# An attention and mixture-of-experts kernel: row-half pairs for the last 64 units of routed tiles, another place for transposes and for normalised rows

## The chip, the cores and the metric

The kernel runs on one core of one Trainium2 chip. The metric is the device time of one execution in microseconds (us); lower is better. The time before is 720.77 us, the median of three runs (720.6 to 722.7).

## The reference

The input x has 16 sequences of 100 tokens with 256 channels (1600 tokens), and each sequence has a context of 361 tokens with 192 channels. All is fp32.

```
x = x + attention(layernorm(x), context)       16 heads of 64; q = x Wq, k, v = context Wkv
                                               softmax(q k^T / 8) v, then Wproj and bproj
h = layernorm(x)
swiglu(h, w1, w2, w3) = (silu(h w1^T) * (h w3^T)) w2^T          704 units
shared = swiglu(h, sw1, sw2, sw3)
p, e   = the largest of 7 sigmoid scores of the router, and its expert
x = x + 0.5 / (0.5 + p) * shared + p / (0.5 + p) * swiglu(h, ew1[e], ew2[e], ew3[e])
```

## The kernel before, in words

**Order of work.** TensorE's order is written out by hand for the whole kernel, and in the attention part those of ScalarE (ACT), VectorE (DVE) and the DMA queue of SyncE (SP) too. Behind the attention, ACT, DVE, SP and GpSimd (POOL) are ordered by a scheduler. All matmul results land in one ring of eight PSUM banks.

**Attention** (L857 to L922) is a loop over 32 steps, s = 2b + g, for batch b and half g of the heads. A step has four score pairs (L688): two 64-row matmuls side by side, whose maxima DVE takes (L701), whose exponentials ACT makes (L704), and which DVE turns in blocks of 32 (L717, for the pair before). Between the score pairs of a step stand the products of keys and values of the next batch (L611). At the end of a step with g = 0 come, in this order on TensorE: the "fillers" (the projection L792 of a finished tile of 128 tokens, and the router's product L245), two units of q (L587) and the products of probabilities with values of batch b-1 (L760).

**Layer norms** run in parts that are spread over the loop. `layer_norm` (L170) gives parts (moments of each tile, roots, and L192, which writes a normalised tile `xn`) and a function `turn`, which transposes the tiles on TensorE (L212) and copies them on ACT into `xT` (L215). One part is taken by `part()` after each of the turned score pairs, so four in a step: after the score pairs i = 1, 2 and 3 are issued and at the step's end. When a group's parts are through, its `turn` is put on the queue `turns`. Groups of tiles: (0, 1) and (2..5) ahead, (6, 7, 8) and (9..12) from step 6 and 9 on for q; and then, for the second half of the layer (`keep`), (0, 1, 2), (3, 4, 5), (6, 7, 8) as the attention finishes them. In the kernel before, `turns` are taken at the beginning of a step with g = 0, behind its first score pair (L899). All normalised tiles share four buffers `xn`.

**Loads.** The context of batch b+2 is loaded at the end of step (b, 1) into one of two buffers `cT` (L917). `load_shared` (L223) loads the first two shared weights `w13_sb` in steps 10 to 13.

**Shared expert** (L984 to L1013): after the attention, `hidden` (L424) and `down` (L493). `down` already takes tiles in pairs for the last 64 units: two matmuls of 64 rows, in the upper and lower half of the array, one for each tile (L499).

**Routed experts** (L1028 to L1093). Tokens are sorted by expert into slot tiles of 128; the number of tiles is found at run time (15 here), and `tc.Switch` branches to code for that number. `fetch` (L949) loads the weights of a slot tile three tiles ahead, 2176 KB. `run(k)` makes on TensorE 8 of 11 unit blocks (L1020, 32 instructions), the transposes of tile k+1 (L979), the last 3 blocks (12 instructions), and then `finish(k-1)`: six matmuls of 128 x 256 (L1032, 12 instructions), the sixth for the last 64 units with 64 rows of zeros, then DVE's sum L1036 and POOL's scattered write L1037. Before the Switch stand `turn(0)`, ahead of the last `down`, and the first 8 blocks of tile 0 (L1087).

Of the kernel before, what the change touches and what calls it, by code (L numbers as in the profile page):

```python
# [14 lines left out]
F32 = mybir.dt.float32  # L15
# [3 lines left out]
ALU = mybir.AluOpType  # L19
# [3 lines left out]
B, LQ, C = 16, 100, 256  # L23
LKV, CTX = 361, 192
H, DK = 16, 64
I, E = 704, 7
P = 128
N = B * LQ
# [18 lines left out]
SINGLE = tuple(t for t in range(NT) if not any(t in p for p in PAIRS))  # L47
NS = (N - E) // P + E
NF = (N + P - 1) // P
WE = 2 * 2 * I + (NI + 1) * C  # L50
QG = 2


# [11 lines left out]
def xattn_moe(  # L65
# [11 lines left out]
    w13: bass.AP,  # L77
    w2: bass.AP,
    wex: bass.AP,
    out: bass.AP,  # L80
):
    nc = tc.nc
# [42 lines left out]
    def bank():  # L125
        return ps.tile([P, 512], F32, tag="mm", name="mm")
# [40 lines left out]

    biases = deque()

    def layer_norm(tiles, keep=False):  # L170


        n = len(tiles)
        of, xns = {}, []

        def moments(i):
            if i == 0:
                of["mv"] = small.tile([P, 4, 2], F32, name="mv")
                of["rstd"] = small.tile([P, 4], F32, name="rstd")
            st = small.tile([P, 6], F32, name="st")  # L180
            nc.vector.bn_stats(st, acc[:, tiles[i], :])
            nc.vector.bn_aggr(of["mv"][:, i, :], st)

        def roots():
            rstd = of["rstd"]
            nc.vector.tensor_scalar(rstd[:, :n], of["mv"][:, :n, 1], EPS, None, ALU.add)
            nc.gpsimd.tensor_tensor(rstd[:, :n], rstd[:, :n], power[:, :n], ALU.pow)

        def normalise(i):
            t = tiles[i]  # L190
            xn = small.tile([P, C], F32, name="xn", bufs=4)
            nc.vector.tensor_scalar(  # L192
                xn,
                acc[:, t, :],
                of["mv"][:, i, 0:1],
                of["rstd"][:, i : i + 1],
                ALU.subtract,
                ALU.mult,
            )
            if keep:  # L200
                nc.sync.dma_start(xn_d[t * P : t * P + rows(t), :], xn[: rows(t), :])
            else:
                biases.append(t)
            xns.append(xn)

        def turn():
            for i in range(0, n, 2):
                tr = bank()
                m = min(2, n - i)
                for o in range(m):  # L210
                    for k in range(2):
                        nc.tensor.transpose(  # L212
                            tr[:, ds((k * m + o) * P, P)], xns[i + o][:, ts(k, P)], ident
                        )
# [296 lines left out]
    with ExitStack() as attn:  # L511
# [34 lines left out]
        def load_later(s):  # L546

            if 1 < s < 4:
                m = ts(s - 2, NCH // 2)
                nc.sync.dma_start(  # L550
                    wp_sb[:, m], wproj.rearrange("(m p) c -> p m c", p=P)[:, m]
                )
            if s == 3:
                nc.sync.dma_start(rb_sb, rbias.to_broadcast([P, E]))
                nc.sync.dma_start(rw_sb[:, :, :E], rwT.rearrange("(k p) e -> p k e", p=P))
            if s == 4 or s == 7:
                load_x(GROUPS[s // 3 + 1])
            if s == 6 or s == 9:
                normalised(GROUPS[s // 3])
            if 10 <= s < 14:  # L560
                load_shared(s - 10)
            if s in (2 * B - 3, 2 * B - 2):
                load_shared(s - 2 * B + 7)

# [234 lines left out]
        turns, fillers, norms = deque(), deque(), deque()  # L799

        def normalised(g, keep=False):
            parts, turn = layer_norm(g, keep)
            norms.extend(parts)


            def turned():
                turn()
                if keep:
                    fillers.append(lambda: norms.extend(router(g)))

            norms.append(lambda: turns.append(turned))
# [31 lines left out]
        pairs = key_pairs(0)  # L843
        product(pairs)
        product(pairs)
        parts, turn_first = layer_norm(FIRST)
        for one in parts:
            one()
        product(pairs)
# [12 lines left out]
        for s, (b, g) in enumerate(steps):  # L862
# [25 lines left out]
            for i in range(n2):  # L888
                exponentials, then = scores(b, g * n2 + i)
                if puts:  # L890
                    puts.popleft()()
                exponentials()
                if turning:
                    turning(tb)
                    part()
                turning = then
                for _ in range(-(-len(pairs) // (n2 - i))):
                    product(pairs)
                while g == i == 0 and turns:  # L899
                    turns.popleft()()  # L900
            if puts:
                puts.popleft()()
            if g == 0:
                while fillers:
                    fillers.popleft()()
                for _ in range(min(2, len(qs))):
                    qs.pop(0)()
# [6 lines left out]
                    after_values()  # L914
                finished(b - 1)
            held.append(moved(tb))
            if g == NG - 1 and b + 2 < B:  # L917
                cTs[b + 2] = load_ctx(b + 2)
            if g == NG - 1:
                host(b)  # L920
# [21 lines left out]

    NW = 4
    wexs = [ew.tile([P, WE], F32, name=f"wex{i}") for i in range(NW)]
    hTs = [ew.tile([P, NI + 1, P], F32, name=f"hgT{i}") for i in range(2)]
    for hT in hTs:
        nc.gpsimd.memset(hT[HALF:, NI, :], 0.0)

    def fetch(k):  # L949

        e = nc.sync.value_load(e_at[:, k : k + 1], min_val=0, max_val=E - 1)
        nc.sync.dma_start(wexs[k % NW], wex[ds(e, 1)].rearrange("o p w -> (o p) w"))

    NX = 4
    xgs, bgs = [], []
    for i in range(NX):
        xgs.append(ew.tile([P, C], F32, name=f"xg{i}"))
        bgs.append(ew.tile([P, C], F32, name=f"bg{i}"))
        nc.gpsimd.memset(xgs[i], 0.0)
        nc.gpsimd.memset(bgs[i], 0.0)  # L960

    def index(k):
        return bass.IndirectOffsetOnAxis(ap=slot_token[:, k : k + 1], axis=0)

    def gather_into(to, of, k):

        nc.gpsimd.indirect_dma_start(
            out=to[k % NX],
            out_offset=None,
            in_=of,  # L970
            in_offset=index(k),
            bounds_check=N - 1,
            oob_is_err=False,
        )
# [9 lines left out]
    with tc.tile_pool(name="hs", bufs=1) as hs:  # L984
# [4 lines left out]
                piece()  # L989
            return hT  # L990

        parts, turn_last = layer_norm(GROUPS[-1], keep=True)
        for one in parts:
            one()
        hT = run_hidden(GROUPS[1])
# [13 lines left out]
        down([(6, hT2, 0), (7, hT2, 1)])  # L1009
        down([(12, hT3, 3)])  # L1010
        down([(9, hT3, 0), (10, hT3, 1)])
        ahead = turn(0)
        down([(8, hT2, 2), (11, hT3, 2)])  # L1013
    hp = ctx.enter_context(tc.tile_pool(name="hp", bufs=2))

# [9 lines left out]
                    stop=(j == 1),  # L1025
                )

    def finish(k, hT, bg):  # L1028
        w = wexs[k % NW]
        y = bank()  # L1030
        for c in range(NI + 1):
            nc.tensor.matmul(  # L1032
                y[:, :C], hT[:, c, :], w[:, ds(4 * I + c * C, C)], start=(c == 0), stop=(c == NI)
            )
        o = hp.tile([P, C], F32, name="o")
        nc.vector.scalar_tensor_tensor(o, y[:, :C], slots[:, k, 1:2], bg, ALU.mult, ALU.add)  # L1036
        nc.gpsimd.indirect_dma_start(  # L1037
            out=out,
            out_offset=index(k),
            in_=o,  # L1040
            in_offset=None,
            bounds_check=N - 1,
            oob_is_err=False,
        )

    def first_products(k, xgT):
        pa, pb = bank(), bank()
        w = wexs[k % NW]
        products(pa, xgT, w, [i * P for i in range(NI - 1)])
        products(pb, xgT, w, [I + HALF + i * P for i in range(NI - 1)])  # L1050
        return pa, pb

    def run(k, state, tiles):


        xgT, last, made = state
        w, hT = wexs[k % NW], hTs[k % 2]
        pa, pb = made or first_products(k, xgT)
        pc = bank()
        n = (NI - 1) * P  # L1060
        s = sp.tile([P, n], F32, name="sg")
        nc.scalar.activation(s, pa[:, :n], AF.Silu)
        nc.vector.tensor_tensor(
# [8 lines left out]
        nc.scalar.activation(s[:, :P], pc[:, :P], AF.Silu)  # L1072
        nc.scalar.activation(s[:HALF, P:], pc[P - HALF :, ts(1, P)], AF.Silu)
        nc.vector.tensor_tensor(hT[:, NI - 1, :], pc[:, ts(2, P)], s[:, :P], ALU.mult)
        nc.vector.tensor_tensor(hT[:HALF, NI, :], pc[:HALF, ts(1, P)], s[:HALF, P:], ALU.mult)
        if last is not None:
            finish(*last)
# [4 lines left out]
        return ahead, (k, hT, bgs[k % NX]), None  # L1082

    n = nc.values_load(e_at[:, NS:], min_val=0, max_val=NS - NF)
    for k in range(NX - 1):
        gather_into(bgs, base_d, k)
    first = ahead, None, first_products(0, ahead)  # L1087

    for extra in tc.Switch(n, NS - NF + 1):
        then = first  # L1090
        for k in range(NF + extra):
            then = run(k, then, NF + extra)
        finish(*then[1])  # L1093


# [52 lines left out]
```

## Time and profile before

| what | value |
| --- | --- |
| median of 3 runs | 720.77 us |
| the profiled execution: own time | 721.24 us |
| its span, first to last instruction | 719.4 us (mean granted TensorE clock 0.995) |
| TensorE (PE) busy | 707.9 us |
| DVE, ACT, POOL busy | 420.5, 280.7, 197.3 us |
| products and steps of the attention | 4.2 to 512.9 us |
| shared expert, sort | to 595.7 us |
| routed experts | 595.7 to 714 us |

How to read it: the timeline lists instructions of one engine in order, merged where alike; its columns are the start in us, the time from there to the end of the last one, engine, line, operation, the tiles, and the count. A part in square brackets is idle time before it and what ended that. Matmuls are pipelined, so the time that a group takes from its neighbours is the distance from its start to the next start. One fp32 matmul is two instructions on TensorE.

### The profile page before, as it was taken

Reading aid. Unit: us, or ns where it says so; the run is one execution under the profiler, and the core shown is the slowest. Engines: PE = TensorE matmul, PEld = TensorE weight load, DVE = VectorE, ACT = ScalarE, POOL = GpSimd, SP = SyncE. Lnnn points to the kernel's source line nnn. Section 1 sums busy time; section 2 is a strip of 40 time slices with the busy share of each in tenths; the row PEclk is TensorE's granted clock in tenths of the full one; section 3 lists DMA queues with packets and bytes.
Section 4 is the critical chain, followed back from the end, with each engine's and each line's share of the span. In section 5 each row is a group of like instructions: output and inputs, shape, how many; then the busy total and the mean of one; then the engine's idle time right before and its main releaser. Section 6 shows DMA issues by size and latency. Waiting matters only on the chain. (4 is left out here: it accounts for less than half of the span.)

```text
span 719.4 us, 14826 instructions
## 1 busy us (share of the span) xinstructions
PE 707.9 (98%) x5192; PEld 510.3 (71%) x5192; DVE 420.5 (58%) x1100; ACT 280.7 (39%) x793; POOL 197.3 (27%) x417
## 2 busy tenths in 40 slices
PE   9999999999999999999999999999999998999996
PEld 6556667667575766757577576755866578999996
DVE  2777766867687576876778778677247222122121
ACT  2564563534545263453644636453022111111110
POOL 4142422322342222323223322233010104343321
PEclk9999999999999999999999999999999999999999
DMA  7055756454474543537354473555104912998860
GB/s 260 23 140 157 178 128 159 95 140 125 106 204 127 166 109 96 139 88 197 93 136 124 109 181 83 142 129 143 52 26 155 382 34 58 326 348 333 309 249 23
DMA packets 55979, 109.23 MB, mean 152 GB/s; under 512 B 28681, under 2 KB 37964, under 8 KB 53972
## 3 DMA queue, kind: packets, MB, share of 16 engines
q1 hardware_dynamic: 45252, 81.79, 37.1%
q0 software_dynamic: 10352, 25.98, 13.8%
q8 instruction: 44, 0.72, 0.4%
q14 instruction: 43, 0.35, 0.2%
q10 hardware_dynamic: 288, 0.39, 0.2%
HBM read 60.81 MB, written 5.35 MB: 92 GB/s over the span
## 5 line engine op out<-in xcount | busy, mean ns | idle before, releaser
L704 ACT ACTIVATE at<-mm,nm 128x361 f32<-128x361 f32 x256 | 142.0, 561 | 173.4 <-DVE nm L701 173.2
L738 POOL DMA_DIRECT2D aT<-tb x256 | 126.1, 500 | 296.7 <-PE mm L760 104.6
L701 DVE TENSOR_REDUCE nm<-mm 128x1 f32<-128x361 f32 x256 | 123.5, 523 | 60.1 <-PE mm L688 59.3
L717 DVE STREAM_TRANSPOSE tb<-at 128x384 f32<-128x384 f32 x256 | 132.9, 558 | 4.5
L611 PE MATMUL mm<-cT,wk_sb 64*128 64x361 f32 x768 | 125.8, 467 | 0.5 <-DMA cT<-in_ctxT 0.4
L611 PE MATMUL mm<-wv_sb,cT 64*128 64x512 f32 (+1 forms) x552 | 126.2, 589 | 0.0
L611 PEld LDWEIGHTS mm<-cT,wk_sb 64*128 64x128 f32 x768 | 75.7, 188 | 45.7 <-issue 5.0
L688 PE MATMUL mm<-kT,qT 64*128 64x361 f32 x512 | 99.2, 479 | 1.7 <-ACT at L704 1.7
L611 PEld LDWEIGHTS mm<-wv_sb,cT 64*128 64x128 f32 (+1 forms) x552 | 53.7, 185 | 53.1 <-issue 43.1
L1020 PE MATMUL mm<-xgT,wex 128*128 128x128 f32 x660 | 78.3, 275 | 0.0
L1020 PEld LDWEIGHTS mm<-xgT,wex 128*128 128x128 f32 x660 | 76.9, 192 | 1.0 <-issue 0.3
L688 PEld LDWEIGHTS mm<-kT,qT 64*128 64x128 f32 x512 | 48.8, 188 | 35.8 <-issue 8.9
L760 PE MATMUL mm<-aT,v 128*64 128x100 f32 (+1 forms) x1472 | 72.5, 251 | 0.5 <-DMA aT<-tb 0.4
L760 PEld LDWEIGHTS mm<-aT,v 128*64 128x64 f32 (+1 forms) x1472 | 67.2, 135 | 4.9 <-issue 3.0
L424 PE MATMUL mm<-xT,w_sb 128*128 128x384 f32 (+1 forms) x176 | 60.9, 503 | 0.0
L424 PEld LDWEIGHTS mm<-xT,w_sb 128*128 128x128 f32 x176 | 32.9, 190 | 26.1 <-issue 8.5
L704 ACT ACTIVATION_READ_ACCUMULATOR at<-mm,nm 128x1 f32 x256 | 50.7, 198 | 0.0
L587 PE MATMUL mm<-xT,wq_sb 128*128 128x200 f32 x256 | 46.9, 336 | 0.0
L587 PEld LDWEIGHTS mm<-xT,wq_sb 128*128 128x128 f32 x256 | 43.4, 190 | 4.0 <-issue 1.5
L792 PE MATMUL mm<-wp_sb,resT 128*128 128x256 f32 x192 | 44.8, 386 | 0.0
L651 ACT COPY kT<-mm 128x361 f32<-128x361 f32 x64 | 29.4, 461 | 39.2 <-PE mm L611 39.2
L792 PEld LDWEIGHTS mm<-wp_sb,resT 128*128 128x128 f32 x192 | 35.9, 191 | 10.3 <-issue 2.5
(154 smaller groups left out, 558.9 us busy)
## 6 DMA issues: line engine op xcount, KB each, us to landing
wex<-in_wex SPq DMA_DIRECT2D x15, 2176.0 KB
aT<-tb POOLq DMA_DIRECT2D x256, 80.2 KB, 3.3
aT<-tb SPq DMA_DIRECT2D x256, 80.2 KB
over<-row SPq DMA_DIRECT2D x64, 100.0 KB
cT<-in_ctxT SPq DMA_DIRECT2D x10, 576.0 KB
cT<-in_ctxT SPq DMA_DIRECT2D x5, 541.5 KB
xn_d<-xn SPq DMA_DIRECT2D x12, 128.0 KB
base_d<-acc SPq DMA_DIRECT2D x12, 128.0 KB
```

Of the source, the lines that this page charges most:

```text
L424: nc.tensor.matmul(to[:, :n], w13_sb[:, k, ds(at, P)], xT[:, k, ds(g[0] * P, n)], start=(k == 0), stop=(k == 1),)
L587: nc.tensor.matmul(pq[:, o, :], wq_sb[:, u, k, ts(o, P)], xT[:, k, ts(g, QG * LQ)], start=(k == 0), stop=(k == 1),)
L611: nc.tensor.matmul(to[o][:height, :width], *operands(o, k), start=(k == 0), stop=(k == NR - 1),)
L651: nc.scalar.copy(kT[:, c, :], to[0][:, :LKV])
L688: nc.tensor.matmul(sc[o][:, :LKV], qTs[b // QG][r, c, ts(b % QG, QB), :], kTs[b][c // 4][r, c % 4, :], start=True, stop=True,)
L701: nc.vector.tensor_reduce(nm[:, o : o + 1], sc[o][:, :LKV], AX.X, ALU.max, negate=True)
L704: nc.scalar.activation(at[:, o, :LKV], sc[o][:, :LKV], AF.Exp, bias=nm[:, o : o + 1], accum_out=sums[:, o : o + 1],)
L717: nc.vector.transpose(tb[:, :, :, o, i * QR : i * QR + 32].rearrange("p j k n -> p k j n"), at[:, o, :].rearrange("p (k j n) -> p k j n", ...
L738: queue.dma_start(aT[ts(j, 32), i].rearrange("p k o n -> p (k o n)"), tb[ts(i, 32), j].rearrange("p k o n -> p (k o n)"),)
L760: nc.tensor.matmul(av[ts(o, DK), i, :], v[:n, ds((2 * c + o) * DK, DK)], aT[:n, :, j, o, ts(i, QR)], start=(j == 0), stop=(j == NJ - 1),)
L792: nc.tensor.matmul(pp[:r, :C], resT[:, c, QP : QP + r], wp_sb[:, c, :], start=(c == 0), stop=(c == NCH - 1))
L1020: nc.tensor.matmul(to[:, ts(o, P)], w[:, ds(j * 2 * I + u, P)], xgT[:, j, :], start=(j == 0), stop=(j == 1),)
```

## The change

1. **Last 64 units of the routed tiles.** `WE` loses one block of 256 columns; the last 64 rows of w2 come in a tensor of their own, `wlast`, twice (both halves of the partitions), by a second DMA in `fetch`. The hidden values of the last 64 units go to `tails`, an even tile into partitions 0 to 63, an odd one into 64 to 127. `finish` makes five blocks and holds an even tile back (unless it is among the last three) until the next tile's five blocks are made; then both tails are multiplied, 64 rows each, and both tiles written.
2. **Transposes in the attention.** `turns` are taken at the end of a step with g = 0, behind the last score pair and ahead of the fillers, but for batch 1, where the place stays.
3. **Normalised tiles for q** are written into `w13_sb`; the four `xn` buffers are left for the kept ones. The loads of `w13_sb` move from steps 10 to 13 to steps 20 to 23.
4. **Context loads** stand at the end of step (b, 0), for b = 0 at (b, 1).
5. **Switch.** `turn(0)` moves behind the last `down` and the load of the tile count; the first 8 blocks of tile 0 move into the branches.

```
-    def layer_norm(tiles, keep=False):
+    def layer_norm(tiles, place=None):
...
-            xn = small.tile([P, C], F32, name="xn", bufs=4)
+            xn = small.tile([P, C], F32, name="xn", bufs=4) if keep else place[:, ts(i, C)]
...
-            if 10 <= s < 14:
-                load_shared(s - 10)
+            if 20 <= s < 24:
+                load_shared(s - 20)
...
+        places = [w13_sb[:, i % 2, :] for i in (1, 0, 1, 0)]
...
-                while g == i == 0 and turns:
+                if b == 1 and g == i == 0:
                     turns.popleft()()
             if puts:
                 puts.popleft()()
             if g == 0:
+                while turns:
+                    turns.popleft()()
                 while fillers:
                     fillers.popleft()()
...
-            if g == NG - 1 and b + 2 < B:
+            if g == (NG - 1 if b == 0 else 0) and b + 2 < B:
                 cTs[b + 2] = load_ctx(b + 2)
...
+        nc.sync.dma_start(wlasts[k % NL], wlast[ds(e, 1)].rearrange("o p w -> (o p) w"))
...
-        ahead = turn(0)
         down([(8, hT2, 2), (11, hT3, 2)])
...
-    def finish(k, hT, bg):
+    def finish(k, hT, tiles):
         w = wexs[k % NW]
         y = bank()
-        for c in range(NI + 1):
+        for c in range(NI):
             nc.tensor.matmul(
-                y[:, :C], hT[:, c, :], w[:, ds(4 * I + c * C, C)], start=(c == 0), stop=(c == NI)
+                y[:, :C], hT[:, c, :], w[:, ds(4 * I + c * C, C)], start=(c == 0), stop=False
             )
+        waiting.append((k, y))
+        if k % 2 == 0 and k < tiles - 3:
+            return
+        for at, y in waiting:
+            r = ts(at % 2, HALF)
+            nc.tensor.matmul(
+                y[:, :C], tails[at // 2 % 2][r], wlasts[at % NL][r], start=False, stop=True
+            )
+        while waiting:
+            at, y = waiting.pop(0)
...
+            nc.vector.scalar_tensor_tensor(o, y[:, :C], slots[:, at, 1:2], bg, ALU.mult, ALU.add)
...
-        nc.vector.tensor_tensor(hT[:HALF, NI, :], pc[:HALF, ts(1, P)], s[:HALF, P:], ALU.mult)
+        tail = tails[k // 2 % 2][ts(k % 2, HALF)]
+        nc.vector.tensor_tensor(tail, pc[:HALF, ts(1, P)], s[:HALF, P:], ALU.mult)
...
-    first = ahead, None, first_products(0, ahead)
+    first = turn(0), None
```

More of the change, by code (lines that the diff above doesn't have):

```diff
@@ L49 @@
 NF = (N + P - 1) // P
-WE = 2 * 2 * I + (NI + 1) * C
+WE = 2 * 2 * I + NI * C
 QG = 2
@@ L79, in xattn_moe @@
     wex: bass.AP,
+    wlast: bass.AP,
     out: bass.AP,
@@ L168, in xattn_moe @@
     biases = deque()
-    def layer_norm(tiles, keep=False):
+    def layer_norm(tiles, place=None):
         n = len(tiles)
+        keep = place is None
         of, xns = {}, []
@@ L801, in normalised @@
         def normalised(g, keep=False):
-            parts, turn = layer_norm(g, keep)
+            parts, turn = layer_norm(g, None if keep else places.pop(0))
             norms.extend(parts)
@@ L845, in xattn_moe @@
         product(pairs)
-        parts, turn_first = layer_norm(FIRST)
+        places = [w13_sb[:, i % 2, :] for i in (1, 0, 1, 0)]
+        parts, turn_first = layer_norm(FIRST, places.pop(0))
         for one in parts:
@@ L944, in xattn_moe @@
     wexs = [ew.tile([P, WE], F32, name=f"wex{i}") for i in range(NW)]
-    hTs = [ew.tile([P, NI + 1, P], F32, name=f"hgT{i}") for i in range(2)]
-    for hT in hTs:
-        nc.gpsimd.memset(hT[HALF:, NI, :], 0.0)
+    hTs = [ew.tile([P, NI, P], F32, name=f"hgT{i}") for i in range(2)]
+    tails = [ew.tile([P, P], F32, name=f"tail{i}") for i in range(2)]
+    NL = 6
+    wlasts = [ew.tile([P, C], F32, name=f"wlast{i}") for i in range(NL)]
     def fetch(k):
@@ L952, in fetch @@
         nc.sync.dma_start(wexs[k % NW], wex[ds(e, 1)].rearrange("o p w -> (o p) w"))
+        nc.sync.dma_start(wlasts[k % NL], wlast[ds(e, 1)].rearrange("o p w -> (o p) w"))
     NX = 4
[L955 to L960, printed above, removed]
+    xgs = [ew.tile([P, C], F32, name=f"xg{i}") for i in range(NX)]
+    bgs = [ew.tile([P, C], F32, name=f"bg{i}") for i in range(NX + 1)]
+    for one in xgs + bgs:
+        nc.gpsimd.memset(one, 0.0)
     def index(k):
@@ L967, in gather_into @@
         nc.gpsimd.indirect_dma_start(
-            out=to[k % NX],
+            out=to[k % len(to)],
             out_offset=None,
@@ L990, in run_hidden @@
             return hT
-        parts, turn_last = layer_norm(GROUPS[-1], keep=True)
+        parts, turn_last = layer_norm(GROUPS[-1])
         for one in parts:
@@ L1026, in products, with run @@
                 )
-    def finish(k, hT, bg):
+    waiting = []
+    def finish(k, hT, tiles):
         w = wexs[k % NW]
         y = bank()
-        for c in range(NI + 1):
+        for c in range(NI):
             nc.tensor.matmul(
-                y[:, :C], hT[:, c, :], w[:, ds(4 * I + c * C, C)], start=(c == 0), stop=(c == NI)
+                y[:, :C], hT[:, c, :], w[:, ds(4 * I + c * C, C)], start=(c == 0), stop=False
             )
[L1035 to L1048, printed above, removed]
+        waiting.append((k, y))
[8 more added lines that the diff above has]
+            at, y = waiting.pop(0)
+            o = hp.tile([P, C], F32, name="o")
+            bg = bgs[at % len(bgs)]
+            nc.vector.scalar_tensor_tensor(o, y[:, :C], slots[:, at, 1:2], bg, ALU.mult, ALU.add)
+            nc.gpsimd.indirect_dma_start(
+                out=out,
+                out_offset=index(at),
+                in_=o,
+                in_offset=None,
+                bounds_check=N - 1,
+                oob_is_err=False,
+            )
+    def run(k, state, tiles):
+        xgT, last = state
+        w, hT = wexs[k % NW], hTs[k % 2]
+        pa, pb, pc = bank(), bank(), bank()
+        n = (NI - 1) * P
         products(pa, xgT, w, [i * P for i in range(NI - 1)])
         products(pb, xgT, w, [I + HALF + i * P for i in range(NI - 1)])
[L1051 to L1060, printed above, removed]
         s = sp.tile([P, n], F32, name="sg")
@@ L1074, in run @@
         nc.vector.tensor_tensor(hT[:, NI - 1, :], pc[:, ts(2, P)], s[:, :P], ALU.mult)
-        nc.vector.tensor_tensor(hT[:HALF, NI, :], pc[:HALF, ts(1, P)], s[:HALF, P:], ALU.mult)
+        tail = tails[k // 2 % 2][ts(k % 2, HALF)]
+        nc.vector.tensor_tensor(tail, pc[:HALF, ts(1, P)], s[:HALF, P:], ALU.mult)
         if last is not None:
-            finish(*last)
+            finish(*last, tiles)
         if k + NX - 1 < tiles:
@@ L1081, in run @@
             fetch(k + NW - 1)
-        return ahead, (k, hT, bgs[k % NX]), None
+        return ahead, (k, hT)
     n = nc.values_load(e_at[:, NS:], min_val=0, max_val=NS - NF)
@@ L1092, in xattn_moe @@
             then = run(k, then, NF + extra)
-        finish(*then[1])
+        finish(*then[1], NF + extra)
 def kernel(**inputs):
@@ L1117 @@
     w13e = w13e.transpose(0, 2, 1, 3).reshape(E, P, 4 * I)
-    w2e = np.pad(w2[1:], ((0, 0), (0, P - HALF), (0, 0))).reshape(E, NI + 1, P, C)
-    w2e = w2e.transpose(0, 2, 1, 3).reshape(E, P, (NI + 1) * C)
+    w2e = w2[1:, : NI * P].reshape(E, NI, P, C).transpose(0, 2, 1, 3).reshape(E, P, NI * C)
     arrays = {
@@ L1132 @@
         "wex": np.concatenate([w13e, w2e], axis=2),
+        "wlast": np.concatenate([w2[1:, NI * P :]] * 2, axis=1),
     }
```

## The prediction

> **What bounds the kernel now.** I read the page first, then TensorE's timeline and its waits, then DVE's and ACT's timelines where TensorE had waited, or would wait after the change.
>
> ```profile
> PE 707.9 (98%) x5192; PEld 510.3 (71%) x5192; DVE 420.5 (58%) x1100; ACT 280.7 (39%) x793; POOL 197.3 (27%) x417
> PEclk9999999999999999999999999999999999999999
> ```
>
> TensorE (PE) is busy for 98% of the span, so nearly everything that it executes, and every wait of it, is time. The page hides the exceptions: the waits name two places of about 2 us. This is the first, in step 14 (PE, then one row of DVE's waits, then two windows):
>
> ```profile
> 224.05 1.09 PE L212 MATMUL mm<-ident,xn 128*128 128x128 f32 x8
> 225.07 0.88 PE L688 MATMUL mm<-kT,qT 64*128 64x361 f32 x4
> 227.69 3.06 PE L688 MATMUL mm<-kT,qT 64*128 64x361 f32 x8 [1.75 <-ACT at L704]
> ...
> DVE xn L192 <- PE mm L212: 3.3, 1, 3.3
> ...
> 224.60:228.00 3.40, 1.65 (x11) 0.91 (x10) 3.37 (x9) 1.01 (x4) 1.28 (x3) 1.00 0.32 97
> 228.00:231.40 3.40, 3.40 (x10) 1.87 (x9) 3.24 (x10) 3.25 (x11) 2.71 (x6) 0.50 0.80 206
> ```
>
> DVE wanted to write a normalised tile, but its xn buffer was waiting for the transposes at 224.05, which PE reached only at the beginning of step 14. DVE stood for 3.3 us, PE then for 1.75, and behind that the granted clock (eighth column) was 0.50 for 3.4 us. Twelve L688 take 1.92 us where nothing is in the way (323.43 to 325.35 below); here 225.07 to 230.69 is 5.62, and the projection behind took 3.9 instead of 3.56: **3.9 us** lost, of which 1.7 (half of 3.4) are the clock.
>
> The decisive view is the end of a step with g = 0. This is step 20, PE, then DVE, then ACT:
>
> ```profile
> 323.43 1.99 PE L688 MATMUL mm<-kT,qT 64*128 64x361 f32 x12
> 325.35 3.72 PE L792 MATMUL mm<-wp_sb,resT 128*128 128x256 f32 x16
> 328.91 2.87 PE L587 MATMUL mm<-xT,wq_sb 128*128 128x200 f32 x16
> ...
> 326.28 0.37 DVE L192 TENSOR_SCALAR xn<-acc,mv,rstd 128x256 f32<-128x256 f32 x1
> 328.60 0.37 DVE L192 TENSOR_SCALAR xn<-acc,mv,rstd 128x256 f32<-128x256 f32 x1
> ...
> 330.51 0.20 ACT L704 ACTIVATION_READ_ACCUMULATOR at<-mm,nm 128x1 f32 x1
> ```
>
> PE issues the three last score pairs in a row and is through with them at 325.35 (call it T). DVE and ACT still work on them: DVE writes normalised tiles at T+1.3 and T+3.62 (ends), ACT ends its last exponential at T+5.36. PE does not feel this lag, because it projects and makes q meanwhile, from things that are long ready.
>
> **Part by part**, against the profiled execution's 721.24 us.
>
> *a. The xn buffers.* Tiles for q no longer share them; the stall of step 14 goes with its clock drop: **-3.9**. What is late next there is part c.
>
> *b. Transposes beside other work of 128 rows.* Now they stand between works of 64 rows. In step 22 the six L212 cost 0.80 (354.42 to 355.22), the twelve products ahead 2.68 instead of 2.58, and the score pairs behind 2.03 instead of 1.92: 1.01 in all. Beside work of 128 rows an instruction takes 0.109 (two transposes from 606.68 to 606.90 in the routed part): 0.66. So 0.35 for each of five moved turns (steps 10, 16, 14, 22, 30 before): **-1.75**.
>
> *c. The moved transposes wait.* By the counting of parts (four a step, in order) they come in steps 10, 12, 14, 20 and 28, at T, ahead of the projection. PE executes in order, so all that follows waits too. At two of the five the last normalised tile is the part behind score pair 2 of the same step, at two others the part behind pair 1.
> - Steps 20 and 28: the third tile is ready at T+3.62 (328.97; 447.96 with T = 444.34), where PE could begin on it at T+0.45: 3.2 each, 6.4. The router behind then finds xT copied.
> - Step 12: the fourth tile is ready at T+1.55 (201.83, T = 200.28); PE has done six transposes at T+0.7: 0.9. The q units behind read older columns.
> - Step 14: third tile at about T+1.6, so 1.1; after 3.56 of projection the router's product (now in this step) needs both copies into xT, which stand on ACT behind the last exponential: T+5.36 + 0.6 + 0.4. PE arrives at T+5.5: 0.9. Together 2.0.
> - Step 10: the tiles are ready, but the q units read tile 6 (tokens 768 to 799). The last exponential ends at 175.18, T = 169.41, and with one copy of 0.6 PE may go on at T+6.4; it arrives at T+0.7+3.56 = T+4.3: 2.1.
>
> Sum **+11.5**. Nothing hides it: PE has no other instruction to take. Bounds: 6.4 (the two long waits alone) and 16 (all five as long).
>
> *d. The clock.* The window of step 14 shows that 1.75 us of idle PE in 3.4 us can bring 3.4 us at half clock; at the Switch 1.99 us, split over two such windows, brought none. The waits of steps 20 and 28 leave PE about 3 us idle within 3.6, that of step 10 2.1 in one piece. I count two drops at 1.7: **+3.4**; ends 0 and 6.8 (four). [...]
>
> *e. Context a step earlier.* In steps 5 and 13 PE waited for cT: the first score pair takes 1.08 (86.11 to 87.19) where it takes 0.71 elsewhere (180.22 to 180.93), and 1.09 in step 13: twice 0.38. Gone: **-0.8**. A load of 576 KB then stands in the DMA queue behind the blocks aT of the half that is used two steps later. If that collides, it is of the size seen in step 12, where L760 takes 4.72 (203.18 to 207.90) for 4.45 in step 10 (175.77 to 180.22): 0.27. The w13 loads in steps 20 to 23 have until step 31; also hidden.
>
> *f. Switch.*
>
> ```profile
> 595.70 3.84 PE L1020 MATMUL mm<-xgT,wex 128*128 128x128 f32 x32
> 601.52 0.41 PE L979 MATMUL mm<-ident,xg 128*128 128x128 f32 x2 [1.99 <-DVE hgT L1063]
> ...
> L1144 PEldq COMPARE_BRANCH x2: 312/1948/3584, 597.7 to 709.7; - x2
> ```
>
> The named releaser had long ended; the branch (597.7 + 3.58 = 601.25) is what PE waited for. PE's sequencer runs some 17 instructions ahead (load of the count at 592.0). After: count at 591.8, 0.74 long, two transposes, branch from about 593.2 to 596.8, under the last `down`; products from about 597.0 for 3.57, next transposes at 600.6 instead of 601.5: **-0.9**. If the branch starts only after the transposes have ended (596.0), it is +1.9.
>
> *g. Routed pairs.* A block of 128 rows costs 0.43 (twelve instructions 608.24 to 610.83: 0.216 each). What two tiles in halves cost, `down` shows:
>
> ```profile
> 590.65 4.48 PE L493 MATMUL mm<-w_sb,hT 128*128 128x256 f32 x20
> 595.07 0.70 PE L499 MATMUL mm<-w_sb,hT 64*128 64x256 f32 x4
> ```
>
> To 595.70 that is 5.05; less 20 x 0.216 = 0.73 for the pair, and a first instruction behind a change of form costs 0.1 more (part b): 0.83, against 0.86 for two blocks. Six pairs: -0.2. A single tile of 64 rows has the same two changes of form: 0.83 against 0.43, twice, and 0.2 at the very end: +1.0. Sum **+0.8**; ends -0.5 and +2 (halves one after the other). [...]
>
> POOL's two writes in a row (out_x, median 6.6 us to landing, each behind the one before) and four gathers of 1.3 us fit in the 15.4 us of two tiles; wlast adds a transfer, but no bytes (2048 + 128 KB). If either cover were gone, DVE's sum would hold a PSUM bank for some us.
>
> **Sum:** -3.9 - 1.75 + 11.5 + 3.4 - 0.8 - 0.9 + 0.8 = +8.35, so 729.6 for an execution like the profiled one. The median of runs lies 0.47 under it: **729.1**.
>
> **Rivals.**
> 1. *Waits as in c, but the clock holds*: 729.1 - 3.4 = 725.7. For it: the drop needs the idle time in one window; against: 3 us is most of one.
> 2. *DVE and ACT keep up* (the other side: faster). One mechanism, at T: if the last tile is normalised within 0.45 us behind T and the copies are not behind the exponentials, c and d vanish: 720.8 - 6.55 = 714.2. Against it: the lag of 3.62 in both long steps, and the order of parts, which the change leaves.
> 3. *Only steps 20 and 28 wait, without clock drops*: 714.2 + 6.4 = 720.6, no difference.
> 4. *More clock drops and an uncovered branch*: four drops (+3.4) and +2.8 from f: 735.
> 5. *The halves don't run side by side* (the pairs don't do what they say): g +2 instead of +0.8, 730.3; within the forecast.
>
> **Chances.** Forecast with one to three drops (726.5 to 732.5, rival 5 included) 0.57; rival 1 with its neighbours (723 to 726.5) 0.19; above 732.5 (rival 4) 0.08; rival 3 (718.6 to 722.9) 0.08; rival 2 0.08. About 0.3% (2.2 us) is what a measurement of this kernel can tell from no change. So slower 0.84, same 0.08, faster 0.08. Range: 722.5 to 733.
>
> **What would show it.** In the profile after: L212 at the end of steps 20 and 28 with 2 us idle ahead of the last transposes, released by DVE's xn; L587 of step 10 and the router of step 14 released by ACT's L215; PEclk digits below 9 there; no stall at step 14's scores; no cT wait in steps 5 and 13; the first transposes in the branch at about 5 us behind the last `down`; routed tiles 0.4 slower at the end. It is wrong if those transposes show no idle time ahead of them.

## The result, and the profile after

The changed kernel took 732.49 us in the median of 6 runs (729.92 to 735.57), the kernel before 721.38 us (719.42 to 722.75) beside it: a ratio of 1.0155, 95% interval 1.0123 to 1.0187. It is slower by 11.1 us, and its runs spread more. The profiled execution took 734.11 us, its span is 732.3 us: 12.87 us more than the profiled execution before.

From the page after, the rows of TensorE and of its granted clock:

```profile
PE 712.7 (97%) x5192; PEld 508.0 (69%) x5192; DVE 422.1 (58%) x1100; ACT 280.5 (38%) x793; POOL 197.0 (27%) x416
PEclk9999999999999999999999998999999999999999
```

PE has as many instructions as before. It is busy for 4.8 us more and idle for 8.1 us more: work became slower, and waits came. One digit of the clock fell below 9. PE's waits (line waited for, sum, times, longest):

```profile
PE mm L214 <- DVE xn L194: 6.5, 5, 2.0
PE mm L762 <- DMA over<-row: 2.0, 1, 2.0
PE mm L589 <- ACT xT L217: 2.0, 1, 2.0
...
PE mm L1026 <- DVE acc L507: 1.0, 1, 1.0
PE mm L214 <- DVE w_sb L194: 0.7, 1, 0.7
PE mm L247 <- ACT xT L217: 0.6, 1, 0.6
```

(Lines stand two higher up to the attention's end: L214 is L212 before, L247 is L245, L589 is L587, L690 is L688, L762 is L760, L794 is L792.) The moved transposes wait for DVE, q and the router behind them for ACT's copies; the stall of step 14's scores and the waits for cT are gone. One wait was not foreseen: 2.0 us of the values L762 for a DMA. The end of step 20 shows the long one, PE first, then two rows of DVE:

```profile
322.71 1.99 PE L690 MATMUL mm<-kT,qT 64*128 64x361 f32 x12
324.63 0.44 PE L214 MATMUL mm<-ident,xn 128*128 128x128 f32 x2
325.98 0.44 PE L214 MATMUL mm<-ident,xn 128*128 128x128 f32 x2 [0.91 <-DVE xn L194]
328.40 0.62 PE L214 MATMUL mm<-ident,xn 128*128 128x128 f32 x2 [1.97 <-DVE xn L194]
328.81 5.14 PE L794 MATMUL mm<-wp_sb,resT 128*128 128x256 f32 x16
...
325.56 0.37 DVE L194 TENSOR_SCALAR xn<-acc,mv,rstd 128x256 f32<-128x256 f32 x1
327.88 0.37 DVE L194 TENSOR_SCALAR xn<-acc,mv,rstd 128x256 f32<-128x256 f32 x1
```

T is 324.63. DVE's tiles are ready at T+1.30 and T+3.62, the times that the prediction read from the trace before. Six transposes take 4.18 us (324.63 to 328.81), where the prediction has 0.66 for six without a wait. The projection behind takes 5.07 (328.81 to 333.88) instead of 3.56, at a granted clock of 0.50 from 328.47 to 331.88. Step 28 waits as long (0.92 and 1.98 us), and its projection takes 6.15. Steps 10 and 30:

```profile
167.86 3.62 PE L794 MATMUL mm<-wp_sb,resT 128*128 128x256 f32 x16
173.43 4.35 PE L589 MATMUL mm<-xT,wq_sb 128*128 128x200 f32 x16 [1.96 <-ACT xT L217]
...
486.94 2.35 PE L762 MATMUL mm<-aT,v 128*64 128x100 f32 x48
491.30 3.01 PE L762 MATMUL mm<-aT,v 128*64 128x100 f32 x43 [2.01 <-DMA over<-row]
```

The clock, in windows whose ends are the times at which the granted clock (eighth column) changes. They lie on one grid of 3.413 us (from 174.86 to 492.29 it is 93 windows); the third column, behind the window and its length, is PE's busy time in the window:

```profile
171.45:174.86 3.41, 1.45 (x9) 1.43 (x9) 2.52 (x8) 1.95 (x6) 0.00 (x0) 1.00 0.16 41
174.86:178.28 3.42, 3.42 (x18) 2.96 (x18) 1.04 (x2) 0.00 (x0) 0.00 (x0) 0.50 0.03 13
...
325.05:328.47 3.42, 0.53 (x4) 0.30 (x4) 3.38 (x10) 1.48 (x6) 0.06 (x1) 1.00 0.77 226
328.47:331.88 3.41, 3.41 (x10) 2.78 (x11) 1.77 (x5) 1.95 (x6) 0.00 (x0) 0.50 0.49 130
...
447.92:451.33 3.41, 1.66 (x10) 0.60 (x6) 3.34 (x10) 2.12 (x8) 1.26 (x3) 1.00 0.86 252
451.33:454.74 3.41, 2.27 (x7) 1.94 (x8) 2.98 (x8) 2.28 (x8) 0.00 (x0) 0.50 0.59 161
454.74:458.16 3.42, 3.42 (x10) 2.70 (x9) 0.00 (x0) 0.06 (x1) 0.00 (x0) 0.50 0.10 32
488.87:492.29 3.42, 1.41 (x32) 1.24 (x30) 3.35 (x10) 1.20 (x4) 0.06 (x1) 1.00 0.76 186
492.29:495.70 3.41, 3.41 (x35) 2.63 (x31) 0.75 (x3) 0.00 (x0) 1.54 (x4) 0.50 0.47 116
```

Up to the last matmul, five windows are at half clock (before: one): behind the waits of steps 10, 20, 28 (two in a row) and 30. Half of PE's busy time in them is (3.42 + 3.41 + 2.27 + 3.42 + 3.41) / 2 = 8.0 us, as an upper estimate of what they cost; by the rows it is some 7.3 (part d below).

**Where the time went**, by the starts of the steps' first score matmuls in both traces (change of a step's length, after less before; predicted terms by their letters):

| place | predicted | measured |
| --- | --- | --- |
| up to the first score pair | none | -0.7 |
| steps 5 and 13 (e) | -0.8 | -0.9 |
| step 10 (c 2.1, b -0.35) | +1.75 | +3.5 |
| steps 12, 14, 16 (a -3.9, c 0.9 + 2.0, b twice -0.35) | -1.7 | -2.5 |
| steps 20, 22 (c 3.2, d 1.7, b -0.35) | +4.55 | +5.1 |
| steps 28, 30 (the same) | +4.55 | +8.55 |
| Switch, to the third transposes (f) | -0.9 | -0.95 |
| from there to the last matmul (g) | +0.8 | +0.8 |
| sum | +8.25 | +12.9 |

Transposes went from step 14 to 12, 16 to 14, 22 to 20, 30 to 28, and within step 10. What is left out (other steps, step 31, the end) cancels within 0.1 us. The predicted sum is 8.25 and not 8.35, because the terms of c add up to 11.4, where the prediction has 11.5.

### The profile page after: what moved, and what is told of

Same layout as the page of the kernel before. It is cut to its first block, busy times and chain, and to the rows that moved or that the text cites. A ratio compares the mean times of both kernels' runs of the same rounds, so it can differ in the third digit from the quotient of the medians.

```text
span 732.3 us, 14864 instructions
## 1 busy us (share of the span) xinstructions
PE 712.7 (97%) x5192; PEld 508.0 (69%) x5192; DVE 422.1 (58%) x1100; ACT 280.5 (38%) x793; POOL 197.0 (27%) x416
## 5 line engine op out<-in xcount | busy, mean ns | idle before, releaser
L613 PEld LDWEIGHTS mm<-cT,wk_sb 64*128 64x128 f32 x768 | 73.9, 187 | 45.8 <-issue 3.0
L690 PE MATMUL mm<-kT,qT 64*128 64x361 f32 x512 | 97.0, 474 | 0.0
L1026 PE MATMUL mm<-xgT,wex 128*128 128x128 f32 x660 | 79.0, 276 | 1.0 <-DVE acc L507 1.0
L1026 PEld LDWEIGHTS mm<-xgT,wex 128*128 128x128 f32 x660 | 76.3, 192 | 3.8 <-issue 3.5
L762 PE MATMUL mm<-aT,v 128*64 128x100 f32 (+1 forms) x1472 | 73.7, 254 | 2.1 <-DMA over<-row 2.0
L762 PEld LDWEIGHTS mm<-aT,v 128*64 128x64 f32 (+1 forms) x1472 | 68.4, 137 | 7.0 <-issue 3.5
L690 PEld LDWEIGHTS mm<-kT,qT 64*128 64x128 f32 x512 | 48.0, 187 | 35.8 <-issue 9.6
L589 PE MATMUL mm<-xT,wq_sb 128*128 128x200 f32 x256 | 48.5, 343 | 2.0 <-ACT xT L217 2.0
L589 PEld LDWEIGHTS mm<-xT,wq_sb 128*128 128x128 f32 x256 | 44.3, 194 | 6.4 <-ACT xT L217 2.4
L794 PE MATMUL mm<-wp_sb,resT 128*128 128x256 f32 x192 | 48.1, 408 | 0.0
L794 PEld LDWEIGHTS mm<-wp_sb,resT 128*128 128x128 f32 x192 | 38.8, 207 | 8.9 <-issue 2.5
```

The lines of the kernel that those rows point to most:

```text
L589: nc.tensor.matmul(pq[:, o, :], wq_sb[:, u, k, ts(o, P)], xT[:, k, ts(g, QG * LQ)], start=(k == 0), stop=(k == 1),)
L613: nc.tensor.matmul(to[o][:height, :width], *operands(o, k), start=(k == 0), stop=(k == NR - 1),)
L690: nc.tensor.matmul(sc[o][:, :LKV], qTs[b // QG][r, c, ts(b % QG, QB), :], kTs[b][c // 4][r, c % 4, :], start=True, stop=True,)
L762: nc.tensor.matmul(av[ts(o, DK), i, :], v[:n, ds((2 * c + o) * DK, DK)], aT[:n, :, j, o, ts(i, QR)], start=(j == 0), stop=(j == NJ - 1),)
L794: nc.tensor.matmul(pp[:r, :C], resT[:, c, QP : QP + r], wp_sb[:, c, :], start=(c == 0), stop=(c == NCH - 1))
L1026: nc.tensor.matmul(to[:, ts(o, P)], w[:, ds(j * 2 * I + u, P)], xgT[:, j, :], start=(j == 0), stop=(j == 1),)
```

## The experiments

**Theory A** is the prediction's: the turning's place costs the time, since DVE and ACT lag behind TensorE there, and half clock follows; the other parts are worth what was worked out. The rivals, other places for the cost, stand in the expectations.

### 1. The turning put back

```diff
-                if b == 1 and g == i == 0:
+                while g == i == 0 and turns:
                     turns.popleft()()
...
-                while turns:
-                    turns.popleft()()
                 while fillers:
```

> The changed kernel with one part undone: transposes are taken at the beginning of a step with g = 0 again. Theory A (the transposes at the step's end wait for DVE and ACT, and the idle time brings clock drops): all waits of steps 10 to 30 and all clock drops of the attention go, and what is left of the change is -3.9 or -2.2 (step 14, with or without its clock drop), -0.8 (context), -0.9 (Switch), +0.8 (pairs): 721.4 before gives 715.5 to 718.5 us. Rival B (the loads in other steps, the pairs or the Switch carry the loss): it stays above 728.

Measured: 714.81 us (before beside it: 719.35), ratio 0.9926 (0.9899 to 0.9952). No window of the attention is at half clock, PE's largest wait behind the start is 0.9 us. That is under the 715.5 to 718.5 of Theory A, but the kernel before beside it is faster too than the 721.4 from which Theory A starts; 0.9926 of 721.4 is 716.1, inside. All parts but the turning, taken together, make the kernel faster; the turning costs some 16.5 us of the changed kernel (1.0155 less 0.9926, of 720 us).

### 2. The turning alone

The kernel before with the opposite edit:

```diff
-                while g == i == 0 and turns:
+                if b == 1 and g == i == 0:
                     turns.popleft()()
...
             if g == 0:
+                while turns:
+                    turns.popleft()()
                 while fillers:
```

> The kernel before with that one part alone: transposes at the end of a step with g = 0. Theory A: the loss is there without any other part, and a little larger, as the 0.8 of the context and the 0.9 of the Switch are not won: 730 to 736 us. The xn stall of step 14 should go here too, since the four tiles of tokens 9 to 12 are now transposed in step 12. Rival B: 720 to 723.

Measured: 732.79 us, ratio 1.0164 (1.0127 to 1.0201), as slow as the whole change. Windows at half clock stand at steps 20, 28 (two) and 30 as in the changed kernel; step 10 has none, the Switch has one. PE's longest wait is the one for DVE's tiles:

```profile
PE mm L212 <- DVE xn L192: 7.2, 6, 2.0
```

Step 14's stall does not occur either, though the tiles for q still share the buffers: the transposes that free them are done at the end of step 12 already. So part a and the turning remove the same stall, and the changed kernel saves it only once (steps 12, 14 and 16 change by -2.5 us here too). That is why the turning costs 16.5 us on top of part a and only 11.8 (1.0164, of 720 us) without it.

### 3. The waits filled with work

```diff
+                if s in (20, 28):
+                    fill(4)
                 while turns:
                     turns.popleft()()
...
+                if s == 10:
+                    fill(2)
                 for _ in range(min(2, len(qs))):
                     qs.pop(0)()
+                if s == 30:
+                    fill(2)
```

`fill(n)` issues n matmuls of 128 x 128 x 512 whose results nobody reads: extra work, to keep PE busy where it waited.

> The changed kernel with unused matmuls (128 x 512, about 0.86 us each, results not read) put where TensorE waited: four ahead of the transposes of steps 20 and 28, two ahead of the q units of step 10, two ahead of the products with values of step 30. The waits for DVE, ACT and DMA end when they ended before, so the matmuls should cost almost nothing by themselves. Theory A with the clock: the five windows at half clock (1.7 us each) of the profiled execution go, 724 to 728 us, granted clock 0.99 or more, digits of 9 throughout. Rival C (the idle gaps don't bring the clock down): 732 to 735, and as many windows. If the waits were overlapped by something else, the eight to twelve matmuls add up to 10 us: 740.

Measured: 727.28 us (726.81 to 727.76), ratio 1.0093 (1.0059 to 1.0126), 5.2 us less than the changed kernel's median (4.5 by the two ratios: the kernel before beside it took 719.35 here and 721.38 there), and no window at half clock up to the last matmul. The runs lie within 0.95 us of each other, where those of the changed kernel spread over 5.65, with the mean granted clock going from 0.994 (729.92 us) to 0.987 (735.57): the clock is also what makes its time unsteady. PE does 24 instructions more and the kernel is faster.

### 4. The turning behind the q units

```diff
             if g == 0:
-                while turns:
-                    turns.popleft()()
                 while fillers:
...
+            while g == 0 and turns:
+                turns.popleft()()
             if g == 0 and s:
                 for at in range(NG):
```

Still between works of 128 rows and ahead of the values L762, but behind the projection and the q units, some 6 us later (3.56 and 2.8). The place is also behind the step's last part of the layer norm, so the transposes of tiles 6, 7 and 8 come in step 8 already, where the changed kernel has them in step 10; and the router's product comes in the next step with g = 0, as before.

> The changed kernel with the transposes at another place of the same step: behind the projection and the q units, ahead of the products with values (the router follows in the next step with g = 0). Theory A: 6 us behind the last score pair DVE has normalised all tiles, so TensorE does not wait, the clock holds, and the transposes still stand beside work of 128 rows: about 1.75 less than with the transposes at the beginning, 713.5 to 716.5 us. Rival B: above 728, as with the changed kernel.

Measured: 713.58 us (712.96 to 713.71), ratio 0.9902 (0.9869 to 0.9934). PE at the end of step 20:

```profile
321.85 2.87 PE L589 MATMUL mm<-xT,wq_sb 128*128 128x200 f32 x16
324.56 0.82 PE L214 MATMUL mm<-ident,xn 128*128 128x128 f32 x6
325.31 4.52 PE L762 MATMUL mm<-aT,v 128*64 128x100 f32 x96
```

Six transposes in 0.75 us without a wait (1.01 between 64-row works before): the saving that the place among 128-row works gives is had, and its price is not paid. Step 30 waits 0.9 us for the DMA, with no drop of the clock.

### 5 to 8. The other parts, each undone on number 4

Number 5 makes six blocks of 128 rows for every routed tile, as before:

```diff
-WE = 2 * 2 * I + NI * C
+WE = 2 * 2 * I + (NI + 1) * C
...
-        nc.sync.dma_start(wlasts[k % NL], wlast[ds(e, 1)].rearrange("o p w -> (o p) w"))
...
-        for c in range(NI):
+        for c in range(NI + 1):
```

> The version with the transposes behind the q units (713.6 us, clock steady), and each routed tile multiplied by six blocks of 128 rows again, as before the change. Theory A, by the drains of the half-row form: -0.75, 712.6 to 713.2 us; in the trace two tiles take 15.44 us on TensorE, as in the kernel before (7.72 each). Rival D (halves side by side at the price of one matmul): +2.6 without them, 716.

Measured: 715.18 us (714.31 to 718.49), ratio 0.9931 (0.9908 to 0.9954), against the expectation of Theory A. The trace shows why: from the third transposes to the last matmul the routed part takes 111.52 us, and in it is one stop, with its half clock behind it:

```profile
613.63 5.24 PE L1023 MATMUL mm<-xgT,wex 128*128 128x128 f32 x32 [3.17 <-ACT xgT L985]
```

(L1023 here is L1026 elsewhere.) ACT began its copy xgT at 613.20, though the transposes had ended by 606.6; the profile names nothing on this core that it waited for. Without the stop (3.17) and the clock (5.07 instead of 3.57 to the next group) the stretch is 106.85 us. The kernel before needs 106.69, number 4 and the changed kernel 107.47. Number 11 below tells whether the stop belongs to the edit.

Number 6 pairs all tiles but the last:

```diff
-        if k % 2 == 0 and k < tiles - 3:
+        if k % 2 == 0 and k < tiles - 1:
```

> The same version with all tiles but the last in pairs (tiles 12 and 13 too). By TensorE's rows one pair takes the place of two singles: -0.8. But the writes of tiles 12 and 13 then follow each other at the very end, each behind the landing of the one before (2.2 us at the end of the kernel before), and the last write waits for both: +1.8. Together +1: 714.0 to 715.0 us. If writes don't wait for each other: 712.8.

Measured: 716.54 us, ratio 0.9944 (0.9927 to 0.9962): slower than expected. PE ends 0.4 us earlier than in number 4 (one more pair), but the last three writes now stand one behind the other. POOL at the end of number 6, then of number 4:

```profile
704.37 0.98 POOL L1058 DMA_INDIRECT out_x<-o,slot_token  x1 [10.84 <-DVE o L1057]
707.56 0.98 POOL L1058 DMA_INDIRECT out_x<-o,slot_token  x1 [2.21 <-DVE o L1057]
710.74 0.98 POOL L1058 DMA_INDIRECT out_x<-o,slot_token  x1 [2.20 <-DMA out_x<-o,slot_token]
```

```profile
696.85 0.98 POOL L1058 DMA_INDIRECT out_x<-o,slot_token  x1 [4.68 <-DVE o L1057]
704.26 0.98 POOL L1058 DMA_INDIRECT out_x<-o,slot_token  x1 [6.43 <-DVE o L1057]
707.44 0.98 POOL L1058 DMA_INDIRECT out_x<-o,slot_token  x1 [2.20 <-DVE o L1057]
```

The last row of number 6 names the write before as what it waited for; writes in a row are 3.2 us apart from start to start in both. Tile 12's write, out at 696.85 in number 4, is held back until tile 13 is made, and the two behind it follow: 3.2 us at the very end, where nothing covers them. Of the two bounds tried, "all but the last three" is the better one.

Number 7 loads the contexts at (b, 1) again:

```diff
-            if g == (NG - 1 if b == 0 else 0) and b + 2 < B:
+            if g == NG - 1 and b + 2 < B:
```

> The same version with the context load at the end of step (b, 1), as in the kernel before. The first score pairs of two steps should wait for cT again: +0.4 to +0.9, 714.0 to 714.5 us, and rows of PE that wait for cT<-in_ctxT. If the earlier load only moved the collision to another transfer: no difference, 713.3 to 713.9.

Measured: 714.43 us, ratio 0.9915 (0.9897 to 0.9932), as expected in size, but the interval holds number 4's ratio too, and the trace speaks against the reason: by the lengths of the steps, step 13 has no wait and step 5 one of 0.13. Number 2, with the loads at the old place as well, has none in either; number 9 has 0.40 and 0.12. All ten traces with the moved load have none. So the move does remove a wait, but one that is there in some executions only: 0.9, 0, 0.13 and 0.52 us in the four traces without it.

Number 8 has the Switch as before, with transposes and 8 blocks of tile 0 ahead of it:

```diff
+        ahead = turn(0)
         down([(8, hT2, 2), (11, hT3, 2)])
...
-    first = turn(0), None
+    first = ahead, None, first_products(0, ahead)
```

> The same version with the Switch as in the kernel before: the first transposes ahead of the last down, 8 blocks of tile 0 ahead of the branch. The branch (3.58 us) then starts only when these blocks have been handed to TensorE: +0.9, 714.2 to 714.8 us, and about 2 us idle ahead of the second transposes. If the branch were hidden in both: 713.6.

Measured: 714.67 us, ratio 0.9918 (0.9901 to 0.9935). From the last values L762 to the third transposes it takes 95.63 us, number 4 92.86. PE in that trace:

```profile
588.23 3.84 PE L1027 MATMUL mm<-xgT,wex 128*128 128x128 f32 x32
594.07 0.41 PE L986 MATMUL mm<-ident,xg 128*128 128x128 f32 x2 [2.00 <-DVE hgT L1085]
```

The uncovered branch costs 2.0 us here as before. This time it fell into one window (1.41 of 3.41 us busy) and brought half clock: 1.6 us more. The rest, some 1.1 us, agrees with f's 0.9.

### 9 to 12. On one chip: part a alone, numbers 4 and 5 again, and parts taken early

Number 9, the kernel before with

```diff
-            xn = small.tile([P, C], F32, name="xn", bufs=4)
+            xn = small.tile([P, C], F32, name="xn", bufs=4) if keep else place[:, ts(i, C)]
...
-            if 10 <= s < 14:
-                load_shared(s - 10)
+            if 20 <= s < 24:
+                load_shared(s - 20)
```

> The kernel before with part a alone: the normalised tiles for q get places in the idle half of the shared experts' weight buffer, and the loads into it come in steps 20 to 23. Theory A (part a's price was right): the stall of step 14 (2.2 us) and the half clock behind it (1.7 us) go and nothing is late next, so 2.2 to 3.9 us faster than before, a ratio of 0.9945 to 0.997. Rival E (the stall only moves, for instance to the next wait of DVE): within 0.2% of before.

Measured: 717.07 us (before beside it: 720.67), ratio 0.9955 (0.9942 to 0.9968), so 3.2 us with an interval of 2.3 to 4.2. In its trace step 14 is 3.96 us shorter than before. The stall and its half clock were what the prediction took them for.

Number 10 is number 4 again.

> The same kernel as e4_turns_late, so that it stands on one chip beside the other three. Both theories: a ratio to before of 0.988 to 0.993, as in e4 (0.9902).

Measured: 714.46 us, ratio 0.9910 (0.9893 to 0.9927). As in number 4.

Number 11 is number 5 again.

> The same kernel as e5_late_nopairs (six blocks of 128 rows for every routed tile). In the trace of e5 the routed products took 0.8 us less than in e4, but TensorE stood 3.2 us once for ACT's copy xgT, with a half clock behind it. Theory A (the stop is a chance of that execution): 0.4 to 1.0 us faster than e10 in the median. Rival F (the stop comes with the six blocks): at least 1 us slower than e10, and the trace shows the stop at the same place.

Measured: 713.74 us (713.30 to 714.67), ratio 0.9909 (0.9892 to 0.9925), 0.7 us under number 10, with no stop in its routed part: from the third transposes to the last matmul it takes 106.69 us, as in the kernel before. So the six blocks run without the stop of number 5 (what held ACT there, and how often it does, stays open), and the routed pairs cost what Theory A says: 0.78 us. The two medians lie within each other's runs; the difference is shown by the traces.

Number 12 is the changed kernel; it leaves the transposes at the changed place and makes their tiles earlier:

```diff
                 exponentials()
+                if s in (12, 14, 20, 28) and i < 2:
+                    part()
                 if turning:
```

> The changed kernel, transposes at the changed place, but two parts of the layer norm more are issued early in steps 12, 14, 20 and 28, so that the last normalised tile stands two score pairs earlier in DVE's order. Theory A (the transposes wait because DVE lags behind TensorE at the last parts): the waits of steps 12, 20 and 28 (1.0, 3.5, 3.5) and most of that of step 14 go, with the half clock of 20 and 28 (some 5 us); the waits of steps 10 and 30 stay, each with its drop of the clock: 717 to 720.5 us, about the time of before. Rival G (the place itself costs the time: transposes between the score pairs and the projection wait for ACT's copies and for banks whatever DVE does): 727 us or more.

Measured: 722.31 us (721.96 to 724.40), ratio 1.0033 (1.0017 to 1.0048), 1.8 us more than Theory A's upper end. PE at the end of step 20:

```profile
320.03 1.99 PE L690 MATMUL mm<-kT,qT 64*128 64x361 f32 x12
321.95 0.87 PE L214 MATMUL mm<-ident,xn 128*128 128x128 f32 x6
322.66 3.62 PE L794 MATMUL mm<-wp_sb,resT 128*128 128x256 f32 x16
327.79 0.54 PE L247 MATMUL mm<-xT,rw_sb 128*32 128x96 f32 x16 [1.51 <-ACT xT L217]
```

The waits for DVE are gone (0.71 us for six transposes), so DVE's order of parts was their cause. But 1.51 us of wait for ACT's copies come in their place (also in step 28; 1.21 in step 14), which the wait for DVE had hidden: the copies stand behind the last exponentials on ACT (the last one ended at T+5.36 in the trace before; the router goes on at T+5.84 here). Both theories hold a part: DVE's lag is 3.5 us a step, and 1.5 of them would be lost to ACT anyway. Only a later place (number 4) is rid of both.

This trace has no drop of the clock, though steps 10 and 30 wait 1.96 and 2.10 us, as in the changed kernel. The two windows that hold most of these waits:

```profile
171.92:175.34 3.42, 1.69 (x10) 1.69 (x11) 2.29 (x8) 1.94 (x6) 0.00 (x0) 1.00 0.13 31
479.12:482.53 3.41, 1.75 (x39) 1.78 (x41) 2.55 (x7) 0.54 (x2) 0.50 (x1) 1.00 0.53 156
```

The grid lies otherwise in this execution: PE is busy for 1.69 and 1.75 us in these windows, where the ones ahead of the drops in steps 10 and 30 of the changed kernel have 1.45 and 1.41.

## Why the prediction was right, and where not

The forecast was 729.1 us, slower; 732.49 was measured, inside the range of 722.5 to 733, at its upper end; three of the six runs lie above the range. The mechanism was right: number 2 shows that the turning alone makes the kernel as slow, number 1 that without it the change is a gain.

- **a (-3.9).** Right: -3.2 (2.3 to 4.2) by itself, -3.96 in the trace (the prediction's own rows add up to 4.0). Its other half was not seen: the moved turning frees the same buffers, so it is no gain over number 2.
- **b (-1.75).** About right where nothing waits: six transposes take 0.71 to 0.75 us in numbers 4 and 12, where six between 64-row works took 1.01 with what they add to their neighbours, so 0.3 for each turn instead of 0.35. At step 30 it is worth nothing (below).
- **c (+11.5).** Right, step by step: 2.0 at step 10 (2.1 foreseen), 1.0 at step 12 (0.9), 1.0 and 0.65 at step 14 (1.1 and 0.9), 3.5 at steps 20 and 28 (3.2; 0.2 of each is clock). "The router behind then finds xT copied" holds only because DVE's wait is the longer one, as number 12 shows.
- **d (+3.4), the step that failed.** The term was mis-sized: "I count two drops at 1.7", but there were five windows at half clock in the profiled execution (the one that the kernel before has is in a). The drop behind step 28 lasted two windows, and steps 10 and 30 had one each. They cost some 7.3 us: the projection takes 1.5 longer than its 3.56 in step 20 and 2.6 longer in step 28; step 10 is 1.6 longer than in number 12, where no drop came; and from the second half of the values to the next product step 30 takes 1.6 longer than there. Number 3 gives 5.2 us by the medians, 4.5 by the ratios. The number of drops is not the same in every run: (1 - granted clock) x span / 1.7 gives, as an estimate, 2.6 windows in the fastest of the six runs and 5.6 in the slowest, part of one of them behind the last matmul. Two drops were the best case, not the middle.
- **A wait that was missed: step 30.** The text says of the moved transposes what is waited for at the new place, and nothing of what they had covered at the old one. Step 30 before (four rows), and the beginning of step 30 after:

```profile
467.54 0.77 PE L688 MATMUL mm<-kT,qT 64*128 64x361 f32 x4
470.81 0.87 PE L212 MATMUL mm<-ident,xn 128*128 128x128 f32 x6
476.22 0.54 PE L245 MATMUL mm<-xT,rw_sb 128*32 128x96 f32 x16
477.14 4.67 PE L760 MATMUL mm<-aT,v 128*64 128x100 f32 x96 [0.38 <-DMA aT<-tb]
...
479.27 0.77 PE L690 MATMUL mm<-kT,qT 64*128 64x361 f32 x4
```

Before, transposes, router and a gap of 0.4 us kept the values L760 back until 9.6 us behind the step's beginning, and their second half until some 11.9. After, they begin at 7.7 us, and the second half is released at 12.0: 2.0 us of wait. (The profile names `over<-row`, which L762 does not read; half of the blocks `aT`, which it does read, come by the same queue ahead of it: in SP's rows `aT` from 482.89, `over<-row` from 487.96.) The work that was moved out of step 30 had stood in the shadow of a transfer, so step 30 gave nothing back for what step 28 took on: without a drop, in number 12, it is 0.2 us longer than before.

- **e (-0.8).** The right size for these two executions (-0.9), by chance in part: without the move the wait is between 0 and 0.9.
- **f (-0.9) and g (+0.8).** Both right: -0.95 and +0.78. The 1.0 us that PE waits at L1026 is in f's sum (596.0 to 597.0). The single tiles carry g's cost; number 6, with a pair in place of two singles, is 0.82 us shorter in that stretch: a pair of tiles takes 5.15 us for its blocks (5.19 before), a single tile 2.98 (2.59). PE at the end after, two single tiles: 2.25 (721.00 to 723.25) and 0.63, and the next five blocks take 2.35, 0.10 more, behind the change of form (the rows show the time, not that it is a drain, as the expectation of number 5 calls it):

```profile
721.00 2.32 PE L1042 MATMUL mm<-wex,hgT 128*128 128x256 f32 x10
723.25 0.70 PE L1050 MATMUL mm<-wlast,tail 64*128 64x256 f32 x2
723.88 2.42 PE L1042 MATMUL mm<-wex,hgT 128*128 128x256 f32 x10
726.23 0.70 PE L1050 MATMUL mm<-wlast,tail 64*128 64x256 f32 x2
```

Rival 1 (the clock holds) was refuted by the windows and by number 3, rival 2 by the waits, rival 3 by steps 10 and 12. Of rival 4 the first half came true: there were more drops, but the branch cost what f says. Rival 5 was refuted by g's 0.78, and by the rows: two matmuls of 64 rows take 0.63 us (x4, 595.07 to 595.70 in the prediction), as one does (x2, 723.25 to 723.88).

The fastest versions are numbers 4 and 10, one kernel (ratios 0.9902 and 0.9910), and number 11 without the pairs (0.9909): 713.6 to 714.5 us.

## What to carry to other kernels

Before work on the bottleneck engine is moved, ask three things in the trace: when its inputs are ready at the new place (here 3.6 us late, in DVE's order of parts), which second input will wait once the first does not (ACT's copies), and which transfer it covered at the old place (step 30). Put such work behind, not ahead of, what is long ready: with the same transposes some 6 us later in the step (and one group two steps earlier) the kernel takes 18 us less (ratios 1.0155 and 0.9902). And price a wait of TensorE with its clock: the Switch's gap of 2.0 us cost 2.0 us in the kernel before and 3.6 in number 8, by where it fell.

## What the runs showed of the hardware

**Which windows brought a drop.** In all 14 profiled executions of this case, between 20 and 700 us from the start, I divided the time by the grid of 3.413 us that the clock's changes show. Every window at full clock in which PE was busy for 1.67 us or less was followed by half clock: 11 windows, 0.53 to 1.67 us (four in the changed kernel, four in number 2, one each in numbers 5 and 8 and in the kernel before; 1.67 is that of the kernel before, 1.65 where the prediction shows it with rounded ends). No window with 1.69 us or more was: 1.69, 1.75, 1.81, 1.91 and upward. The ends of matmuls are modelled in the records, so a difference of 0.02 us can't be told. At half clock, two windows with 2.3 us of busy time (step 28 of the changed kernel and of number 2) were followed by another at half clock, those with 2.9 us or more by full clock. The first half-clock windows of the drops in the profiled execution after begin 45.0, 36.0 and 12.0 windows apart (174.86, 328.47, 451.33 and 492.29). Single gaps of 1.75 us (step 14 before) and of 1.96 and 2.01 us (steps 10 and 30 after) brought a drop.

So a gap of 2.0 us cost the clock in some of these executions and not in others. If every position of the grid is as likely, the part of the positions that leave more than 1.72 us of it in one window (3.41 less the 1.69 above) is, as an estimate from these windows, (3.41 + 2.0 - 2 x 1.72) / 3.41 = 0.58. The wait of step 10 brought a drop in the changed kernel and none in numbers 2 and 12; that of the Switch brought one in numbers 2 and 8 and none in the kernel before and number 9.

**Unused matmuls can pay for themselves** where PE would wait anyway: number 3, with 12 of them, is 4.5 to 5.2 us faster.
